# Layer 0 of a two-layer conv-attention kernel: row sums with ones as weights on four column tiles and one transpose, behind the first three steps of the next block; second x loaded later

## The chip, the cores and the metric

The kernel runs on one core of a Trainium2 chip. The metric is the device time of one execution in microseconds (us), the median of three runs. Engines are named as in the profile: PE is TensorE (matmuls), PEld its loading of weights, DVE is VectorE, ACT is ScalarE, POOL is GpSimd, SP is SyncE, which here does nothing but issue transfers. PSUM is the memory that PE writes its products to, one bank a tile.

## What is computed

All data are float32. The input x has 4 images of 128 channels and 64 x 64 = 4096 positions. Layer 0, the one that is changed, is an attention over positions without heads:

```python
def _L0_conv_ref(x, w1, b1, a1, w2, b2, a2, wa, ba, aa):
    e1 = _conv1x1(x, w1, b1, a1).reshape(N, -1, HW)     # 64 x 4096 for each image
    e2 = _conv1x1(x, w2, b2, a2).reshape(N, -1, HW)     # 64 x 4096
    asm = _conv1x1(x, wa, ba, aa).reshape(N, C, HW)     # 128 x 4096
    score = jnp.einsum('nci,ncj->nij', e1, e2)
    score = jax.nn.softmax(score, axis=2)
    out = jnp.einsum('nij,ncj->nci', score, asm)
    return out.reshape(N, C, H, W)
...
x = x + _L0_conv_ref(_gn(x), ...)
t = _to_tokens(x)
t = t + _L1_attn_ref(_ln_t(t), L1_attn_W_kv, L1_attn_q_proj)
t = t + _L1_ffn_ref(_ln_t(t), ...)
```

`_gn` is a group norm, `_ln_t` a layer norm over channels, `_conv1x1` a 1x1 convolution with a leaky ReLU. The softmax's row sums, one for each of the 4096 positions i of an image, are what this change is about. Layer 1 (an attention with cumulative sums, then a mixture of experts) is as before.

## The kernel before

**Blocks and steps.** Layer 0 (`layer0`) walks over 4 images b and, in each, over 8 blocks qb of 512 positions i (`BLK`). A block has 16 steps p (`NPR`), and a step takes 256 positions j. `steps` is the list of all 512 of them and n its index. In a step, `weigh` (L1929) adds to the two accumulators `av` in PSUM: four matmuls of 64 rows, which are 8 matmul instructions, since a float32 matmul is two. Then `probs` (L1909), for the step two ahead, makes the scores `sc` on PE (two matmuls of 64 rows, 4 instructions), their exponentials `pr` on ACT (L1919), and adds them into `acc` on DVE (L1926, a copy at L1923 for a block's first step). `acc` has two halves of 512 columns; the softmax's row sum of a position is the sum of its column over both halves and all 128 partitions. There is no maximum subtracted.

**Block end.** At step 15, `collect` (L1943) moves `av` to `o` (a copy on ACT, L1946, and an addition on DVE, L1947) and adds the halves of `acc` into `sums` (L1950, one buffer). Then `row_sums` runs for the block before, whose name is `done`: four times a 128 x 128 piece of `sums` is loaded as weights and a column of ones is moved through it (L1965), which leaves the sums of 128 positions in one column of `pd`; DVE copies the four columns to `rows` (L1968) and takes `inv`, their reciprocals (L1970). After that comes the block's share of preparing the next image: `project` (L1858: `pe`, `y`, `z`, `e1`, `e2`, with two transfers from SBUF to SBUF on SP) and `value` (L1883: `pa`, `ya`, `za`, `am`), one of each at nearly every block end of images 0 to 2. At the block ends of image 3 there are instead the first keys and tokens of layer 1 (`keys`, L968, matmul `f_pk`, and `tokens`, L961, transposes `f_ltr`). Last comes `finish` (L1973) for `done`: four transposes of `o` into `ptr` (named `otr` in the profile, L1977), and four operations on DVE (L1979) that scale by `inv`, add the input `xr` and write `t`. `fetch` (L1953) then loads `xr` for the block that just ended, and that block becomes `done`.

**Order.** The order on PE is the order of the program text (`manual_schedule` for PE). The orders on DVE, ACT, POOL and SP are chosen by a planner when the program is built, from what it expects to be ready, with the place in the text as the priority; they are then fixed, and each engine runs its own in order.

**Buffers that matter.** PSUM tag `sm` (one bank) holds `pd`, `pa` and, in image 3, the small tiles of layer 1's scan; tag `x` (one bank) holds `pe`, `otr`, `f_ltr` and the scan's rows; tag `kv` (two) holds `sc` and `f_pk`; `av` has one bank for each of its two halves. In SBUF `sums`, `xr` and the input image `x` have one buffer each, `xn` and `o` two, `pr` three. `load_x(b + 1)` writes over the image before, so it waits for the last `normal` (L1850, `xn`) that reads it.

**Scan and close.** In image 3, `point()` runs layer 1's small scan operations at p = 3, 7, 11 and at the block end. `tile_stats` and `close_stats` (L254, L259) take the layer norm's statistics of finished rows of `t`.

**Last block.** Behind the loop, two `later` calls put `row_sums` and `finish` of the very last block behind two `keys`, at the next `point()`.

Of the kernel before, what the change touches and what calls it, by code (L numbers as in the profile page):

```python
# [13 lines left out]
P = 128  # L14
# [3 lines left out]
def conv_attn_hybrid_kernel(  # L18
# [24 lines left out]
    nc = tc.nc  # L43
# [8 lines left out]
    NBLK = N // BLK  # L52
    CPB = BLK // P
# [8 lines left out]
    ident = const.tile([P, P], F32, tag="ident", name="ident")  # L62
# [3 lines left out]
    ones = const.tile([P, 1], F32, tag="ones", name="ones")  # L66
# [179 lines left out]
    rows = resid.tile([P, B * NCH], F32, tag="rows", name="rows")  # L246
# [7 lines left out]
    def tile_stats(pool, b, i):  # L254
        st = pool.tile([P, 6], F32, tag="l1_st", name=f"l1_st_{b}_{i}", bufs=4)
        nc.vector.bn_stats(st, t[:, b * NCH + i, :])
        nc.vector.bn_aggr(ln_mv[:, b, i, :], st)
# [570 lines left out]
    def fast():  # L828
# [18 lines left out]
        def later(delay, fn):  # L847
            env.tasks.append((env.now + delay, fn))

        def point():  # L850
            env.now += 1
            due = [f for at, f in env.tasks if at <= env.now]
            env.tasks = [(at, f) for at, f in env.tasks if at > env.now]
            for f in due:
                f()
# [920 lines left out]
        def layer0(env):  # L1776
            ps, one, big = env.ps, env.one, env.big
            with ExitStack() as l0:
# [5 lines left out]
                def load_x(b):  # L1784
                    xs = one.tile([P, N], F32, tag="x", name=f"x_{b}")
                    parts = 8 if b == 0 else 4
                    for q in range(parts):
                        cols = bass.ts(q, N // parts)
                        eng = nc.scalar if b == 0 and q % 2 else nc.sync
                        eng.dma_start(out=xs[:, cols], in_=x[b, :, cols])  # L1790
                    return xs

                xs_of = {0: load_x(0)}
# [111 lines left out]
                NPR = NCH // 2  # L1905
                steps = [(b, qb, p) for b in range(B) for qb in range(NBLK) for p in range(NPR)]
                acc_of, av_of, o_of, prep = {}, {}, {}, {}

                def probs(b, qb, p):  # L1909
                    e1, e2, _ = made[b]  # L1910
                    cols = bass.ts(qb, BLK)
                    sc = ps.tile([P, 2, BLK], F32, tag="kv", name=f"sc_{b}_{qb}_{p}", bufs=2)
                    for u in range(2):
                        nc.tensor.matmul(  # L1914
                            sc[:, u, :], e2[halves[u], p, :], e1[halves[u], cols],
                            start=True, stop=True,
                        )
                    pr = tmp.tile([P, 2, BLK], F32, tag="pr", name=f"pr_{b}_{qb}_{p}", bufs=3)
                    nc.scalar.activation(pr, sc, AF.Exp)  # L1919
                    if p == 0:  # L1920
                        acc = small.tile([P, 2, BLK], F32, tag="acc", name=f"acc_{b}_{qb}")
                        acc_of[b, qb] = acc
                        nc.vector.tensor_copy(acc, pr)  # L1923
                    else:
                        acc = acc_of[b, qb]
                        nc.vector.tensor_add(acc, acc, pr)  # L1926
                    return pr
# [31 lines left out]

                def row_sums(b, qb):  # L1960
                    o, sums, xr = o_of[b, qb]
                    at = bass.ts(b * NBLK + qb, CPB)
                    pd = ps.tile([P, BLK], F32, tag="sm", name=f"pd_{b}_{qb}")
                    for c in range(CPB):
                        nc.tensor.matmul(  # L1965
                            pd[:, c : c + 1], sums[:, bass.ts(c, P)], ones, start=True, stop=True
                        )
                    nc.vector.tensor_copy(rows[:, at], pd[:, :CPB])  # L1968
                    inv = tmp.tile([P, CPB], F32, tag="inv", name=f"inv_{b}_{qb}")
                    nc.vector.reciprocal(inv, rows[:, at])  # L1970
                    o_of[b, qb] = (o, inv, xr)

                def finish(b, qb):  # L1973
                    o, inv, xr = o_of.pop((b, qb))
                    ptr = ps.tile([P, CPB, C], F32, tag="x", name=f"otr_{b}_{qb}")
                    for c in range(CPB):
                        nc.tensor.transpose(ptr[:, c, :], o[:, bass.ts(c, P)], ident)  # L1977
                    for c in range(CPB):
                        nc.vector.scalar_tensor_tensor(  # L1979
                            out=t[:, b * NCH + qb * CPB + c, :], in0=ptr[:, c, :],  # L1980
                            scalar=inv[:, c : c + 1], in1=xr[:, c, :], op0=ALU.mult, op1=ALU.add,
                        )
# [11 lines left out]
                done, todo = None, []  # L1994
                env.xl_pool = lambda name: tmp.tile([P, CPB, C], F32, tag="xn", name=name)
                for n, (b, qb, p) in enumerate(steps):
                    weigh(b, qb, p, queue.pop(0))
                    if (b, qb) == (0, 0) and p % 2 == 0 and p // 2 + 2 < NBLK:
                        k = p // 2 + 2
                        normal(k)  # L2000
                        project(k)
                        value(k)
                        if k == NBLK - 1:
                            xs_of[1] = load_x(1)
                    if b + 1 < B:
                        first = 1 if b == 0 else 0
                        if qb == first:
                            if p == 0:
                                prep[b + 1] = preparation(b + 1)
                                todo = list(range(NBLK))  # L2010
                            stat, chain, normal, project, value = prep[b + 1]
                            if 1 <= p <= NBLK:
                                stat(p - 1)
                            elif p == NBLK + 1:
                                chain[0]()
                            elif p in (11, 13):
                                chain[(p - 9) // 2]()
                            elif p == 15:
                                normal(0)
                    if b > 0 and 2 <= qb < 6 and p % 2 == 0:  # L2020
                        tile_stats(tmp, b - 1, (qb - 2) * NBLK + p // 2)
                    if b > 0 and (qb, p) == (6, 3):
                        close_stats(b - 1)
                    if b == B - 1 and qb > 0 and p % 4 == 3 and p < NPR - 1:
                        point()
                    if n + 2 < len(steps):
                        queue.append(probs(*steps[n + 2]))
                    if p == NPR - 1:
                        collect(b, qb)
                        if done:  # L2030
                            row_sums(*done)
                        mine = []
                        if todo:
                            left = NBLK - qb
                            mine = [todo.pop(0) for _ in range(-(-len(todo) // left))]
                        for k in mine:
                            _, _, normal, project, value = prep[b + 1]
                            project(k)
                            value(k)
                            if k + 1 < NBLK:  # L2040
                                normal(k + 1)
                            elif b + 2 < B:
                                xs_of[b + 2] = load_x(b + 2)
                            else:
                                env.hold_weights()
                        if b == B - 1:
                            if qb == 0:
                                env.first_rooms()
                                normals(0)
                                tokens(0)  # L2050
                            elif qb <= LAG:
                                for c in range(CPB):
                                    keys(qb - 1, c)
                                tokens(qb)
                            if qb < LAG:
                                normals(qb + 1)
                            point()
                        if done:
                            finish(*done)
                        fetch(b, qb)  # L2060
                        done = (b, qb)
                later(1, lambda: row_sums(*done))
                later(1, lambda: finish(*done))
                keys(LAG, 0)
                keys(LAG, 1)
                point()

        def last_root():
# [257 lines left out]
```

## Time and profile before

| what | value |
|---|---|
| time, median of three runs | 2317.12 us (2316.6 to 2318.71) |
| the profiled execution: its own time | 2323.74 us |
| its span, first to last instruction | 2322.0 us |
| PE busy | 2247.8 us, 97% of the span |
| DVE, ACT, POOL busy | 62%, 47%, 8% |
| mean granted TensorE clock | 0.992 |
| layer 0, up to the last `finish` | about 1533 us of the span |
| `av` matmuls, L1939 | 4096, 978.0 us |
| `sc` matmuls, L1914 | 2048, 534.4 us |
| `pd` matmuls, L1965 | 256, each 167 to 271 ns |
| `otr` transposes, L1977 | 128, each 272 to 329 ns |
| `sums` waits for `pd`, on DVE | 16.3 us in 30 waits |

A PE length in the profile runs from the start of a matmul to its modelled end; matmuls overlap, so a step's cost is read from the distance between starts. In a run of plain steps, the 8 `av` take 1.72 us from first start to the next group's start, and the 4 `sc` take 0.86 us. A form such as 64*128 means weights of 64 rows and 128 columns; PE runs two such side by side, four with 32 columns (128*32), and one at a time with 128*128.

### The profile page before, as it was taken

Reading aid. Unit: us, or ns where it says so; the run is one execution under the profiler, and the core shown is the slowest. Engines: PE = TensorE matmul, PEld = TensorE weight load, DVE = VectorE, ACT = ScalarE, POOL = GpSimd, SP = SyncE. Lnnn points to the kernel's source line nnn. Section 1 sums busy time; section 2 is a strip of 40 time slices with the busy share of each in tenths; the row PEclk is TensorE's granted clock in tenths of the full one; section 3 lists DMA queues with packets and bytes.
Section 4 is the critical chain, followed back from the end, with each engine's and each line's share of the span. In section 5 each row is a group of like instructions: output and inputs, shape, how many; then the busy total and the mean of one; then the engine's idle time right before and its main releaser. Section 6 shows DMA issues by size and latency. Waiting matters only on the chain.

```text
span 2322.0 us, 43150 instructions
## 1 busy us (share of the span) xinstructions
PE 2247.8 (97%) x18352; PEld 1168.5 (50%) x18352; DVE 1444.6 (62%) x2361; ACT 1086.4 (47%) x1324; POOL 175.9 (8%) x364
## 2 busy tenths in 40 slices
PE   7999999999999999999999999999999999999997
PEld 3544444444444444444444444456565556556663
DVE  7666565655665565565556656568777677865623
ACT  2343333433333443334455444455666566566641
POOL 0000000000000000000000000012211222122311
PEclk9999999999999999999999999999999999999989
DMA  2000010000010000000000000011122121114578
GB/s 77 32 12 17 9 45 8 17 8 9 17 45 9 9 17 9 9 25 27 9 5 5 10 5 5 20 44 41 41 58 53 43 59 46 52 47 129 153 279 303
DMA packets 78555, 104.77 MB, mean 45 GB/s; under 512 B 8976, under 2 KB 44816, under 8 KB 78352
## 3 DMA queue, kind: packets, MB, share of 16 engines
q1 hardware_dynamic: 77264, 99.81, 14.0%
q8 instruction: 146, 2.39, 0.4%
q0 software_dynamic: 512, 1.05, 0.2%
q10 hardware_dynamic: 576, 1.05, 0.1%
q14 instruction: 57, 0.47, 0.1%
HBM read 78.55 MB, written 17.04 MB: 41 GB/s over the span
## 4 chain that ended last, share of the span: by engine, by line
PE 86%; DVE 6%; ACT 3%; DMA 3%; issue 1%; SPq 0%; POOL 0%; another core or an unknown queue 0%; ACTq 0%; DVEq 0%; POOLq 0%
PE av L1939 36%; PE sc L1914 18%; PE f_pv L1128 9%; PE f_pk L973 8%; PE f_pt L1151 3%; PE f_po L1174 2%; PE pd L1965 1%; DMA x<-in_x_dram 1%; ACT f_e1a L980 1%; PE pa L1887 1%; PE pe L1861 1%; PE f_po L1186 1%; DVE f_e1a L981 1%; DVE f_e1a L982 1%; PE f_pl L1291 1%
## 5 line engine op out<-in xcount | busy, mean ns | idle before, releaser
L1939 PE MATMUL av<-pr,am 64*128 64x512 f32 x4096 | 978.0, 592 | 2.9 <-ACT pr L1919 2.9
L1919 ACT ACTIVATE pr<-sc 128x1024 f32<-128x1024 f32 x512 | 523.6, 1023 | 782.7 <-PE sc L1914 769.8
L1926 DVE TENSOR_TENSOR acc<-acc,pr 128x1024 f32<-128x1024 f32 x480 | 586.6, 1222 | 485.4 <-ACT pr L1919 481.1
L1939 PEld LDWEIGHTS av<-pr,am 64*128 64x128 f32 x4096 | 401.6, 187 | 472.9 <-issue 457.9
L1914 PE MATMUL sc<-e,e 64*128 64x512 f32 x2048 | 534.4, 591 | 4.7 <-DMA e<-side 4.7
L1914 PEld LDWEIGHTS sc<-e,e 64*128 64x128 f32 x2048 | 201.6, 187 | 236.6 <-issue 229.0
L1128 PE MATMUL f_pv<-f_held,f_ama 128*32 128x256 f32 x4096 | 242.7, 387 | 5.5 <-ACT f_e1a L980 4.5
L973 PE MATMUL f_pk<-f_held,f_ama 128*128 128x512 f32 x512 | 234.9, 603 | 0.0
L1133 ACT ACTIVATE f_amb<-f_pv 128x1024 f32<-128x1024 f32 x128 | 130.8, 1023 | 141.7 <-PE f_pv L1128 140.9
L981 DVE TENSOR_TENSOR f_e1a<-f_e1a,f_held 128x1024 f32<-128x1024 f32 x128 | 157.5, 1231 | 46.6 <-ACT f_e1a L980 46.2
L980 ACT ACTIVATE f_e1a<-f_pk 128x1024 f32<-128x1024 f32 x128 | 129.9, 1025 | 117.8 <-PE f_pk L973 57.8
L1128 PEld LDWEIGHTS f_pv<-f_held,f_ama 128*32 128x32 f32 x4096 | 131.3, 111 | 102.2 <-issue 15.1
L982 DVE TENSOR_REDUCE f_e1a<-f_e1a 128x8 f32<-128x1024 f32 x128 | 155.3, 1218 | 3.5
L973 PEld LDWEIGHTS f_pk<-f_held,f_ama 128*128 128x128 f32 x512 | 92.5, 190 | 109.1 <-issue 101.4
L1092 POOL COPY f_held<-f_e1a 32x32 f32<-32x32 f32 x128 | 30.5, 238 | 924.1 <-DVE f_e1a L1074 563.3
L1151 PE MATMUL f_pt<-f_amb,f_held 128*32 128x128 f32 x1920 | 83.0, 276 | 0.8 <-ACT f_amb L1133 0.8
L918 POOL MEMSET f_held<- 128x1024 f32 x1 | 1.0, 956 | 1036.3 <-DVE xn L1852 1036.3
L1151 PEld LDWEIGHTS f_pt<-f_amb,f_held 128*32 128x32 f32 x1920 | 59.9, 109 | 10.3 <-issue 5.2
L1192 DVE TENSOR_TENSOR t<-t,f_po 128x512 f32<-128x512 f32 (+1 forms) x33 | 22.1, 671 | 55.6 <-PE f_po L1186 55.6
L956 ACT ACTIVATE f_xl<-t,ln_nb,ln_rs 128x128 f32<-128x128 f32 x128 | 52.8, 490 | 0.8 <-PE pa L1887 0.8
L1272 ACT ACTIVATE f_x<-t,f_gnb,f_grs 128x128 f32<-128x128 f32 x126 | 51.3, 482 | 0.4 <-DVE f_gnb L1253 0.4
L1923 DVE COPY acc<-pr 128x1024 f32<-128x1024 f32 x32 | 22.2, 694 | 39.3 <-ACT pr L1919 39.3
(287 smaller groups left out, 1776.6 us busy)
## 6 DMA issues: line engine op xcount, KB each, us to landing
f_e2a<-f_rd SPq DMA_DIRECT2D x128, 128.0 KB, 2.9
xr<-in_xtok_dram SPq DMA_DIRECT2D x32, 256.0 KB, 3.0
f_table<-f_x SPq DMA_DIRECT2D x62, 128.0 KB, 1.8
out_dram<-t SPq DMA_DIRECT2D x14, 512.0 KB, 3.8
x<-in_x_dram SPq DMA_DIRECT2D x12, 512.0 KB, 7.0
e<-e SPq DMA_DIRECT2D x32, 128.0 KB, 2.2
f_ama<-f_rd SPq DMA_DIRECT2D x16, 256.0 KB, 3.8
f_e1b<-f_rd SPq DMA_DIRECT2D x16, 256.0 KB, 6.0
```

Source lines behind the costliest of these rows:

```text
L956: nc.scalar.activation(xl[:, c, :], t[:, b * NCH + i, :], AF.Identity, bias=ln_nb[:, b, i : i + 1], scale=ln_rs[:, b, i : i + 1],)
L973: nc.tensor.matmul(pk[:, i, :], xt_at(n)[:, bass.ts(c, P)], env.wks[:, bass.ts(i, BLK)], start=True, stop=True,)
L980: nc.scalar.activation(flat, pk.rearrange("p i x -> p (i x)"), AF.Silu)
L981: nc.vector.tensor_mul(ks, ks, env.qb)
L982: nc.vector.tensor_reduce(s[:, (n % GB) * CPB + c, :], ks, AX.X, ALU.add)
L1128: nc.tensor.matmul(pv[a * CH : (a + 1) * CH, i, :], xt_at(m)[:, bass.ts(c * NA + i, CH)], env.wvs[:, bass.ts(a, HH * C)], start=True, stop ...
L1133: nc.scalar.activation(env.amb[:, bass.ts(c, HD)], pv.rearrange("p i x -> p (i x)"), AF.Silu)
L1151: nc.tensor.matmul(env.pt[i * CH : (i + 1) * CH, :], lhs, rhs, start=i not in env.begun, stop=False, skip_group_check=True,)
L1914: nc.tensor.matmul(sc[:, u, :], e2[halves[u], p, :], e1[halves[u], cols], start=True, stop=True,)
L1919: nc.scalar.activation(pr, sc, AF.Exp)
L1926: nc.vector.tensor_add(acc, acc, pr)
L1939: nc.tensor.matmul(av, am[h, j, :], pr[h, u, :], start=(j == 0), stop=(j == NCH - 1))
```

## The change

`row_sums` is split in two. The first part loads a 128 x 32 array of ones as weights (a broadcast of the column `ones`) and moves the four 128-column pieces of `sums` through it. Each piece's result goes to another 32 partitions of `pd`, so the four matmuls use four column tiles of PE. DVE then copies the 128 x 128 result back into `sums`. The second part, `row_turn`, transposes that once on PE and copies every 32nd column to `rows`, then takes the reciprocals. The two parts and `finish` leave the block end: they run behind `weigh` of steps 1, 2 and 3 of the next block, one in each, for the block that has just ended. For the last block they lie around the two `keys`. The load of the second image moves in the text from step 10 of the first block to step 13.

```diff
                 def row_sums(b, qb):
                     o, sums, xr = o_of[b, qb]
-                    at = bass.ts(b * NBLK + qb, CPB)
                     pd = ps.tile([P, BLK], F32, tag="sm", name=f"pd_{b}_{qb}")
                     for c in range(CPB):
+                        rows_ = slice(c * (P // CPB), (c + 1) * (P // CPB))
                         nc.tensor.matmul(
-                            pd[:, c : c + 1], sums[:, bass.ts(c, P)], ones, start=True, stop=True
-                        )
-                    nc.vector.tensor_copy(rows[:, at], pd[:, :CPB])
+                            pd[rows_, :P], ones.to_broadcast([P, P // CPB]), sums[:, bass.ts(c, P)],
+                            start=True, stop=True,
+                        )
+                    nc.vector.tensor_copy(sums[:, :P], pd[:, :P])
+                    o_of[b, qb] = (o, sums, xr, pd)
+
+                def row_turn(b, qb):
+                    o, sums, xr, pd = o_of[b, qb]
+                    at = bass.ts(b * NBLK + qb, CPB)
+                    nc.tensor.transpose(pd[:, P : 2 * P], sums[:, :P], ident)
+                    nc.vector.tensor_copy(rows[:, at], pd[:, P : 2 * P : P // CPB])
                     inv = tmp.tile([P, CPB], F32, tag="inv", name=f"inv_{b}_{qb}")
                     nc.vector.reciprocal(inv, rows[:, at])
                     o_of[b, qb] = (o, inv, xr)
...
                         value(k)
-                        if k == NBLK - 1:
-                            xs_of[1] = load_x(1)
...
+                    if done and 1 <= p <= 3:
+                        (row_sums, row_turn, finish)[p - 1](*done)
                     if n + 2 < len(steps):
                         queue.append(probs(*steps[n + 2]))
+                    if n == NPR - 3:
+                        xs_of[1] = load_x(1)
                     if p == NPR - 1:
                         collect(b, qb)
-                        if done:
-                            row_sums(*done)
...
-                        if done:
-                            finish(*done)
                         fetch(b, qb)
                         done = (b, qb)
-                later(1, lambda: row_sums(*done))
                 later(1, lambda: finish(*done))
                 keys(LAG, 0)
+                row_sums(*done)
                 keys(LAG, 1)
+                row_turn(*done)
                 point()
```

## The prediction

> **What bounds the kernel.** I read the chain of waits first.
>
> ```profile
> PE 86%; DVE 6%; ACT 3%; DMA 3%; issue 1%; SPq 0%; POOL 0%; another core or an unknown queue 0%; ACTq 0%; DVEq 0%; POOLq 0%
> ```
>
> PE ends nearly everything, so the change is worth what it does to the order of starts on PE. Next come PE's starts around one block end of image 0 (columns: start, length, engine, line, operation, count; distances between starts are what counts).
>
> ```profile
> 263.83 1.02 PE L1914 MATMUL sc<-e,e 64*128 64x512 f32 x4
> 264.78 1.05 PE L1965 MATMUL pd<-ones,sums 128*128 128x1 f32 x8
> 265.69 1.10 PE L1861 MATMUL pe<-xn,w 128*128 128x512 f32 x2
> 266.78 1.13 PE L1887 MATMUL pa<-was,xn 128*128 128x128 f32 x8
> 267.75 0.60 PE L1977 MATMUL otr<-ident,o 128*128 128x128 f32 x4
> 268.28 1.99 PE L1939 MATMUL av<-pr,am 64*128 64x512 f32 x8
> 270.10 1.02 PE L1914 MATMUL sc<-e,e 64*128 64x512 f32 x4
> ```
>
> PE has no gap. Against the plain pace (sc 0.86, av 1.72) the block end costs 0.09 on the way out of the 64-row form (0.95 - 0.86), pd 0.91, pe 1.09, pa 0.97, otr 0.53, and 0.10 on the way back (av 1.82 instead of 1.72): 3.69 us. pd is eight weight loads at 0.11 each.
>
> **What is left of a block end.** In the first block pe and pa stand alone between steps:
>
> ```profile
> 27.61 1.12 PE L1861 MATMUL pe<-xn,w 128*128 128x512 f32 x2
> 28.57 1.05 PE L1887 MATMUL pa<-was,xn 128*128 128x128 f32 x8
> 29.55 1.13 PE L1914 MATMUL sc<-e,e 64*128 64x512 f32 x4
> ```
>
> So 0.09 + 0.96 + 0.98 + 0.10 = 2.13, and the removal is worth 3.69 - 2.13 = 1.56 us. The next av needs the old accumulators copied out: ACT ends its copy at 264.61 and DVE its addition at 265.33, while PE would come to av at 264.78 + 1.94 = 266.72. That stays hidden; without pe and pa it would cost some 0.6.
>
> **What three visits cost.** Nothing is hidden here: each visit stands in PE's order between av and sc, and pays the way out and back. The trace has a lone transpose in just that place:
>
> ```profile
> 1386.07 1.88 PE L1939 MATMUL av<-pr,am 64*128 64x512 f32 x8
> 1387.88 0.33 PE L1026 MATMUL f_str<-ident,f_e1a 128*128 128x128 f32 x1
> 1388.14 1.13 PE L1914 MATMUL sc<-e,e 64*128 64x512 f32 x4
> 1389.11 1.45 PE L1939 MATMUL av<-pr,am 64*128 64x512 f32 x6
> ```
>
> av takes 1.81, the transpose 0.26, sc 0.97: 0.09 + 0.26 + 0.11 = 0.46. That is row_turn. finish alone is otr where nothing precedes it, 0.59 (1222.56 to 1223.15 below), with 0.20 around it: 0.78. The new row_sums has no row of its own; the nearest has the same form, weights of 32 columns and 128 moved:
>
> ```profile
> 1539.78 1.08 PE L1151 MATMUL f_pt<-f_amb,f_held 128*32 128x128 f32 x32
> 1540.68 0.51 PE L1174 MATMUL f_po<-f_amb,f_e2a 128*32 128x128 f32 x12
> ```
>
> 32 instructions in 0.90. Their single starts lie in fours, 7 ns apart, the second four 0.135 behind the first and the others 0.109 apart. pd's eight are two fours: 0.135 + 0.02 + 0.20 from the last start to the next form's (as from f_eo's last, 2230.33, to f_htr, 2230.53) = 0.355, with 0.20 around it 0.55. Bounds: if pairs on one column tile follow each other, 8 x 0.107 = 0.86, 0.5 more; below 0.3 it can't go, since two fours of 128 columns and a drain remain. I take 0.355, the same form. Sum of visits: 0.55 + 0.46 + 0.78 = 1.79.
>
> The Trainium skill's "TensorEngine Tiling (Array Packing)", Key Properties, says that changing the tiling mode drains the engine; that speaks against this change, which makes three such pairs of changes out of one, and the rows price it at 0.20 a pair. The skill's "TensorE: Matmul & The Clock Gate", Part 3, gives a packed set as one matmul's duration plus some 4 ns a tile; two sets one after the other, at 0.273 each, would be an estimated 0.57 instead of 0.355, or 31 x 0.21 = 6.7 us more in all.
>
> **Sum by kinds of block.** Images 0 to 2 have 22 block ends with one pe and pa: 22 x (1.79 - 1.56) = **+5.1**. The end of the second block has two of each; there otr waits for pe's bank (1.1) behind ACT, and pd to the last otr take 7.04 (126.54 to 133.58). Without pd and otr 4.2 remain (0.96, 0.98, 1.27, 1.0): -2.83 + 1.79 = **-1.0**. Image 3 looks like this:
>
> ```profile
> 1212.85 1.05 PE L1965 MATMUL pd<-ones,sums 128*128 128x1 f32 x8
> 1213.77 7.11 PE L973 MATMUL f_pk<-f_held,f_ama 128*128 128x512 f32 x16
> 1220.72 0.60 PE L965 MATMUL f_ltr<-ident,f_xl 128*128 128x128 f32 x4
> 1222.56 0.66 PE L1977 MATMUL otr<-ident,o 128*128 128x128 f32 x4 [1.25 <-ACT f_ama L966]
> 1223.15 1.99 PE L1939 MATMUL av<-pr,am 64*128 64x512 f32 x8
> ```
>
> Here otr needs the bank that f_ltr holds until ACT has copied it. That wait goes: 0.91 + 1.85 + 0.59 less 0.55 for f_ltr and 0.05 for a cold f_pk is 2.75, against 1.79: -0.95. What is late next is ACT: behind the keys it has four normals (1.64) and a table load (1.28) and starts the next pr at 1226.27. Its keys can start only 0.5 earlier (it waited 0.47 for f_pk), so pr ends at 1226.7 while av of step 2 wants it at 1226.3: a new wait of 0.5 (0 to 0.5). Five blocks at -0.45: **-2.3**. Image 3's first end has f_ltr alone (1.31): -2.22 + 1.79 = **-0.4**. In the seventh, f_ur keeps the wait for the bank: **-0.3**. In three blocks the scan has an operation at step 3, and finish shares its way out and back: **-0.6**. At the very end pd, otr, keys, pd, otr take 6.19 (1526.37 to 1532.56); keys 1.8, pd 0.5, keys 1.8, turn 0.13, otr 0.7 make 4.9, and I keep **-1.2**, since sums is free on DVE right behind the last acc (1525.3).
>
> That is +5.1 - 1.0 - 2.3 - 0.4 - 0.3 - 0.6 - 1.2 = -0.7. Layer 0 also has four PE waits of its own: 1.2 at 331 and 0.7 at 693 (DVE stands in stats for an image's transfer, and acc and pr come late), and 0.7 each at 458 and 819 (two table loads of close_stats). Four t operations (1.4 us of DVE) leave the queue ahead of them; close_stats moves with finish into the image's first block, where DVE is emptier. They may go, or grow by as much: -3.3 to +3. I take **-0.9**.
>
> **DVE, ACT, queues.** DVE gets one copy of 128x128 a block (0.29 by f_e1b at L1168), and loses its 0.54 wait of sums for pd; it idles 1.35 us of each 2.58 us step, so this costs nothing. The one new wait on PE is row_turn's for that copy. PE is 0.96 + 1.72 + 0.09 = 2.8 us from the sc behind pd to the transpose; the copy needs 0.29 and at most the 1.22 of an acc in progress. ACT gets nothing. On SP, fetch's transfer only becomes free earlier, and finish passes no queue. The **second x** goes at zero: its transfers were issued at 54.51, right behind the xn that frees the buffer (53.93), although their place in the text is behind av of 62.28, and the first xr went at 10.71 with a place behind 83. The place in the text does not hold SP; the buffer does. If it did hold, the PE wait between 64 and 75 (0.48 + 2.28 + 0.75, DVE in stats while z, ya and e are due) would go: -3.5.
>
> All in all -0.7 - 0.9 = -1.6 us on the profiled 2323.74 (span 2322.0); on the median of 2317.12 that is **2315.5**. Own range 2310.5 to 2321: the ACT wait and all four stalls gone (-2.5, -2.4), or the stalls doubled (+3.9) and a tenth of the visits at the upper price.
>
> **Rivals.** (1) *The x load really comes later*, -3.5 more: 2312. For it: the text moved; against: 10.71 and 54.51. Chance 0.18. (2) *row_turn waits on DVE.* If the planner's order puts the copy behind acc of step 3, it ends 2.15 + 1.22 + 0.29 = 3.7 behind sc's start (sc to acc by 261.25, 262.35, 263.40), 0.9 after PE comes to the transpose, with av and sc queued behind it. In all 31 blocks +28, 2343; it makes the kernel slower by more than 0.2% from seven blocks on, and in ten gives 2323. For it: the order is fixed beforehand and DVE is behind in the blocks where an image lands; against: pd is done 2 us before that pr. Chance 0.17. (3) *The four column tiles do not run together*: 0.86 instead of 0.355, 31 x 0.5 = +15.6, 2331; f_pt and f_eo speak against. Chance 0.08. The forecast has 0.52; 0.05 is for none of these.
>
> **How the numbers follow.** About 0.2% (4.6 us) is what a measurement of this kernel tells from no change: 2312.5 to 2321.7. The forecast spreads 0.13 faster, 0.33 same, 0.06 slower; rival 1 gives 0.13 faster and 0.05 same; rival 2 0.13 slower and 0.04 same; rival 3 0.08 slower; the rest 0.03 faster, 0.02 slower. Together 0.29, 0.42, 0.29. The range 2309.5 to 2323 leaves out rival 3, most of rival 2 and little below.
>
> **What would show it.** Starts on PE: pe right behind sc at block ends, 2.13 there; visits of 0.55, 0.46 and 0.78; pd's eight starts in two fours; no idle time before row_turn; otr's waits for f_ama gone and up to 0.5 on pr in image 3; x's second transfer still at 54.5. A visit over 0.7 for pd, waits before row_turn, or an unmoved block end would make this wrong.

## The result, and the profile after

| | before | after |
|---|---|---|
| time, median of 22 runs each on one chip | 2320.03 us (2313.64 to 2325.55) | 2321.34 us (2317.01 to 2326.75) |
| after / before | | 1.0005, 95% interval 0.9997 to 1.0013 |
| profiled execution: own time, span | 2323.74, 2322.0 | 2318.04, 2316.3 |
| layer 0, up to the start of the first `f_pv` (L1128) | 1532.56 | 1533.28 |

The change makes no difference that can be measured. The forecast was that, at 2315.5 against the 2317.12 shown, -1.6; measured is +1.3 between the medians.

The profiled execution after is 5.7 us shorter, but not in layer 0. From the first `f_pv` to the end, where both programs have the same work, the two profiles need 789.45 and 783.03, and the seven other profiles below spread over 783.0 to 790.5. So layer 0 is compared by its own end, which is a far finer ruler: a regular block repeats to 0.01 us from block to block and from profile to profile. From here on a block is the distance from its first `av` to the first `av` of the next, and blocks are numbered 0 to 31 through the four images.

PE's waits between 20 and 1535 us add up to 18.0 before and 10.6 after, while layer 0 got no shorter: what was saved in waits was spent on PE. The next view is PE's timeline at the same block end of image 0 that the prediction showed, and the three visits behind it (start, length, engine, line, operation, count):

```profile
266.55 1.02 PE L1914 MATMUL sc<-e,e 64*128 64x512 f32 x4
267.50 1.12 PE L1861 MATMUL pe<-xn,w 128*128 128x512 f32 x2
268.46 1.05 PE L1887 MATMUL pa<-was,xn 128*128 128x128 f32 x8
269.45 1.99 PE L1939 MATMUL av<-pr,am 64*128 64x512 f32 x8
...
272.13 1.88 PE L1939 MATMUL av<-pr,am 64*128 64x512 f32 x8
273.94 0.42 PE L1965 MATMUL pd<-sums,ones 128*32 128x128 f32 x8
274.30 1.13 PE L1914 MATMUL sc<-e,e 64*128 64x512 f32 x4
275.26 1.88 PE L1939 MATMUL av<-pr,am 64*128 64x512 f32 x8
277.07 0.33 PE L1975 MATMUL pd<-ident,sums 128*128 128x128 f32 x1
277.33 1.13 PE L1914 MATMUL sc<-e,e 64*128 64x512 f32 x4
278.29 1.88 PE L1939 MATMUL av<-pr,am 64*128 64x512 f32 x8
280.11 0.66 PE L1985 MATMUL otr<-ident,o 128*128 128x128 f32 x4
280.69 1.13 PE L1914 MATMUL sc<-e,e 64*128 64x512 f32 x4
```

At the block end `pe` now follows `sc` directly: 0.09 + 0.96 + 0.99 + 0.10 = 2.14. Each visit shows the same two surcharges: the `av` ahead of it takes 1.81 or 1.82 instead of 1.72, the `sc` behind it 0.96 instead of 0.86. Between them `pd` takes 0.36, the transpose 0.26, `otr` 0.59 (0.589 by its single starts). A regular block went from 44.90 to 45.15.

Block 6 is one of the two in which the input of a later image arrives. PE's timeline there (in brackets idle time and what ended it):

```profile
320.41 1.88 PE L1939 MATMUL av<-pr,am 64*128 64x512 f32 x8
324.16 0.33 PE L1975 MATMUL pd<-ident,sums 128*128 128x128 f32 x1 [1.87 <-DVE sums L1969]
```

and DVE's at the same place:

```profile
319.05 1.22 DVE L1926 TENSOR_TENSOR acc<-acc,pr 128x1024 f32<-128x1024 f32 x1
321.95 1.96 DVE L1829 BATCH_NORM_STATS2 stats<-x 128x6 f32<-128x512 f32 x3 [1.68 <-DMA x<-in_x_dram]
323.83 0.27 DVE L1969 COPY sums<-pd 128x128 f32<-128x128 f32 x1
```

`pd` is ready at 319.5, but in DVE's fixed order its copy stands behind three `stats`, and these wait for the image's transfer. PE comes to the transpose at 322.2 and stands until the copy is done.

Image 3, the same place as in the prediction:

```profile
1228.17 0.60 PE L965 MATMUL f_ltr<-ident,f_xl 128*128 128x128 f32 x4
1228.70 1.99 PE L1939 MATMUL av<-pr,am 64*128 64x512 f32 x8
...
1233.20 0.42 PE L1965 MATMUL pd<-sums,ones 128*32 128x128 f32 x8
1233.55 1.13 PE L1914 MATMUL sc<-e,e 64*128 64x512 f32 x4
1234.71 1.99 PE L1939 MATMUL av<-pr,am 64*128 64x512 f32 x8
1236.63 0.33 PE L1975 MATMUL pd<-ident,sums 128*128 128x128 f32 x1
```

with ACT's `pr` at the same place:

```profile
1233.63 2.12 ACT L1919 ACTIVATE pr<-sc 128x1024 f32<-128x1024 f32 x2
```

`otr`'s wait of 1.25 for `f_ama` is gone from the block end. In its place `sc` at 1233.55 takes 1.16 to the next start and `av` 1.92, which is 0.2 and 0.1 more than in image 0 above: PE waits a little for `pr`, the first of which ACT starts only at 1233.63, behind the keys, and ends at about 1234.65.

### The profile page after: what moved, and what is told of

It reads as the page before. It is cut to its first block, busy times and chain, and to the rows that moved or that the text cites. A ratio compares the mean times of both kernels' runs of the same rounds, so it can differ in the third digit from the quotient of the medians.

```text
span 2316.3 us, 43180 instructions
## 1 busy us (share of the span) xinstructions
PE 2249.5 (97%) x18384; PEld 1132.1 (49%) x18384; DVE 1455.5 (63%) x2393; ACT 1086.5 (47%) x1324; POOL 177.1 (8%) x364
## 4 chain that ended last, share of the span: by engine, by line
PE 89%; DVE 4%; ACT 3%; DMA 2%; issue 1%; SPq 0%; ACTq 0%; DVEq 0%
PE av L1939 38%; PE sc L1914 20%; PE f_pv L1128 9%; PE f_pk L973 8%; PE f_pt L1151 3%; PE f_po L1174 2%; PE pe L1861 1%; PE pa L1887 1%; PE f_po L1186 1%; DMA x<-in_x_dram 1%; PE otr L1985 1%; PE f_pl L1291 1%; PE f_ltr L965 1%; ACT f_e1a L980 1%; PE f_ph L1665 1%
## 5 line engine op out<-in xcount | busy, mean ns | idle before, releaser
L1939 PEld LDWEIGHTS av<-pr,am 64*128 64x128 f32 x4096 | 395.3, 187 | 475.0 <-issue 462.9
L1914 PEld LDWEIGHTS sc<-e,e 64*128 64x128 f32 x2048 | 190.5, 187 | 211.0 <-issue 202.4
L1128 PE MATMUL f_pv<-f_held,f_ama 128*32 128x256 f32 x4096 | 241.3, 385 | 5.5 <-ACT f_e1a L980 4.5
L1128 PEld LDWEIGHTS f_pv<-f_held,f_ama 128*32 128x32 f32 x4096 | 130.7, 111 | 101.2 <-issue 13.4
L1887 PEld LDWEIGHTS pa<-was,xn 128*128 128x128 f32 x256 | 34.3, 196 | 17.8 <-issue 14.4
```

What stands on the lines that cost most here:

```text
L1128: nc.tensor.matmul(pv[a * CH : (a + 1) * CH, i, :], xt_at(m)[:, bass.ts(c * NA + i, CH)], env.wvs[:, bass.ts(a, HH * C)], start=True, stop ...
L1887: nc.tensor.matmul(pa[:, c, :], xn[:, bass.ts(c, P)], was, start=True, stop=True)
L1914: nc.tensor.matmul(sc[:, u, :], e2[halves[u], p, :], e1[halves[u], cols], start=True, stop=True,)
L1939: nc.tensor.matmul(av, am[h, j, :], pr[h, u, :], start=(j == 0), stop=(j == NCH - 1))
```

## The experiments

One theory stood at the start. **Theory V**: each visit costs 0.2 us for leaving the 64-row form and coming back, so what the cheaper arithmetic gains, the three visits spend. Its rivals put the cost into the new arithmetic itself, or into waits on DVE. Each experiment's layer 0 is read at the start of its first `f_pv`; the ratio is to the kernel before, in runs on the same chip. The edits are shown against the changed kernel, with less important parts left out.

| kernel | layer 0, us | against before | ratio of times, 95% interval |
|---|---|---|---|
| before | 1532.56 | | |
| after | 1533.28 | +0.72 | 1.0005, 0.9997 to 1.0013 |
| 1: two visits | 1522.23 | -10.33 | 0.9944, 0.9930 to 0.9957 |
| 2: at the block's end | 1514.74 | -17.82 | 0.9929, 0.9916 to 0.9943 |
| 3: move only | 1533.03 | +0.47 | 1.0006, 0.9997 to 1.0015 |
| 4: x really held | 1535.81 | +3.25 | 1.0012, 1.0003 to 1.0021 |
| 5: copy on ACT | 1528.67 | -3.89 | 0.9987, 0.9978 to 0.9996 |
| 6: mixed | 1508.54 | -24.02 | 0.9904, 0.9888 to 0.9919 |
| 7: all at the end | 1507.78 | -24.78 | 0.9894, 0.9879 to 0.9909 |

Each row is one profile, and not all of a difference is the edit's. In eight of the nine profiles the granted TensorE clock, the share of full speed that PE is allowed, is 0.5 for a stretch of 3.4 us in layer 0 (experiment 1 has none, experiment 4 two), which costs up to 1.7. These are the kernel before, in two windows, and the changed one (window, length, PE busy and matmuls, granted clock, DMA share, GB/s):

```profile
70.26:73.67 3.41, 3.41 (x20) 1.00 0.13 29
1484.13:1487.55 3.42, 3.42 (x9) 0.50 0.00 0
```

```profile
70.26:73.67 3.41, 3.41 (x10) 0.50 0.07 16
```

The stretch lies in block 31 before, in block 0 with the change and in experiments 3, 5, 6 and 7, in block 17 in experiment 2, and in blocks 1 and 14 in experiment 4. Each begins during PE waits that add up to 1.8 to 3.8 us, or at most 1.3 behind them. But waits of 1.8 to 2.6 occur without such a stretch too, so what brings it about is open.

**Experiment 1: two visits instead of three.**

```diff
-                    if done and 1 <= p <= 3:
-                        (row_sums, row_turn, finish)[p - 1](*done)
+                    if done and p == 1:
+                        row_sums(*done)
+                    if done and p == 2:
+                        row_turn(*done)
+                        finish(*done)
```

> The changed kernel, with finish in the same visit as row_turn (behind step 2) instead of one of its own behind step 3. Theory V (a visit costs 0.09 on the way out, 0.10 on the way back, and an own start of some 0.1 behind the transpose): turn and otr together take 0.16 + 0.53 + 0.20 = 0.89 instead of 0.46 + 0.78 = 1.24, -0.35 in 28 blocks and -0.15 in the three where finish shared the scan's step: layer 0 10 us shorter, time 2311 against 2321 for the changed kernel on the same chip. Rival (the price lies in the instructions, the switches are hidden by the weight loads): 0 to -2. Rival (DVE): four t operations one step earlier make acc late, a new PE wait of up to 1 in each block: +10 or more.

PE's timeline, the joint visit:

```profile
272.55 1.88 PE L1939 MATMUL av<-pr,am 64*128 64x512 f32 x8
274.36 0.33 PE L1975 MATMUL pd<-ident,sums 128*128 128x128 f32 x1
274.53 0.60 PE L1985 MATMUL otr<-ident,o 128*128 128x128 f32 x4
275.06 1.13 PE L1914 MATMUL sc<-e,e 64*128 64x512 f32 x4
```

The transpose is followed after 0.17 and not 0.26, `otr` after 0.53, and only one pair of surcharges is paid. Every regular block is 44.80 instead of 45.15, -0.35 as worked out, with the same instructions on PE. Layer 0 is 11.05 shorter than with the change, of which 0.99 arose in block 0, where this profile has no stretch at half clock, and 0.30 ahead of it; blocks 1 to 31 give 9.8 against the expected 10. Theory V holds. No wait on DVE came with it in the regular blocks, so that rival is out.

**Experiment 2: the new arithmetic, not moved.** Images 0 to 2 have all three parts at the block's end; `pd` takes a bank of tag `kv` there, because `pa` has the one of `sm`.

```diff
-                    if done and 1 <= p <= 3:
+                    if done and b == B - 1 and 1 <= p <= 3:
                         (row_sums, row_turn, finish)[p - 1](*done)
...
                         collect(b, qb)
+                        if done and b < B - 1:
+                            row_sums(*done, at_end=True)
...
+                        if done and b < B - 1:
+                            row_turn(*done)
+                            finish(*done)
                         fetch(b, qb)
```

> The new arithmetic without the move in images 0 to 2: row_sums, row_turn and finish are at the block's end again (pd in a bank of sc's pair, so that it does not collide with pa); image 3 as in the changed kernel. Theory V: the end of a regular block is 0.09 + 0.36 + 0.96 + 0.98 + 0.16 + 0.53 + 0.10 = 3.18 against 3.69 before and 2.13 + 1.79 = 3.92 in the changed kernel: block 44.4 against 44.90 and 45.15, layer 0 about 16 us shorter than with the change (22 x -0.74, the waits of row_turn where an image lands, 4 us, gone, old waits of 2 and the bank wait of the second block, 1.1, back). Rival (the arithmetic is what costs and the move is neutral): block at 45.0 or more. Rival (row_turn waits for DVE, which stands in the addition of the accumulators and in acc): 0.3 to 1.2 a block lost again, block 44.7 to 45.6.

PE's timeline at a block end:

```profile
262.06 1.02 PE L1914 MATMUL sc<-e,e 64*128 64x512 f32 x4
263.01 0.42 PE L1968 MATMUL pd<-sums,ones 128*32 128x128 f32 x8
263.37 1.13 PE L1861 MATMUL pe<-xn,w 128*128 128x512 f32 x2
264.33 1.05 PE L1887 MATMUL pa<-was,xn 128*128 128x128 f32 x8
265.22 0.27 PE L1978 MATMUL pd<-ident,sums 128*128 128x128 f32 x1
265.33 0.60 PE L1988 MATMUL otr<-ident,o 128*128 128x128 f32 x4
265.86 1.99 PE L1939 MATMUL av<-pr,am 64*128 64x512 f32 x8
```

The block end costs 0.09 + 0.36 + 0.96 + 0.89 + 0.11 + 0.53 + 0.10 = 3.04, even less than the 3.18 expected, since instructions of the 128-column form follow each other without a gap. A regular block is 44.25. Both rivals are out: the arithmetic saves 0.65 a block where it stands among its like, and `row_turn` never waits for its copy, which DVE has made while PE is in `pe` and `pa`.

Against the change layer 0 gained 18.5, and would have gained more but for blocks 9 and 17 (46.78 and 48.39). ACT's timeline in block 9 shows why:

```profile
446.78 1.02 ACT L1919 ACTIVATE pr<-sc 128x1024 f32<-128x1024 f32 x1 [3.53 <-PE sc L1914]
447.82 1.28 ACT L260 ACT_TABLE_LOAD   x1
451.43 0.32 ACT L260 ACTIVATE ln_rs<-ln_mv,eps 128x32 f32<-128x32 f32 x1 [2.32 <-DVE ln_mv L257]
451.77 1.28 ACT L1919 ACT_TABLE_LOAD   x1
```

`close_stats` (L259) takes its root when an image's last rows are finished, and with `finish` at the block's end that is one block later. In ACT's fixed order the root stands ahead of the next `pr` and waits 2.32 for the last `ln_mv`. PE waits 2.26 for that `pr` in both blocks; the 1.61 that block 17 is longer is the stretch at half clock, from 811.58.

**Experiment 3: the old arithmetic, moved.**

```diff
-                            pd[rows_, :P], ones.to_broadcast([P, P // CPB]), sums[:, bass.ts(c, P)],
-                            start=True, stop=True,
+                            pd[:, c : c + 1], sums[:, bass.ts(c, P)], ones, start=True, stop=True
...
-                    if done and 1 <= p <= 3:
-                        (row_sums, row_turn, finish)[p - 1](*done)
+                    if done and p == 1:
+                        row_sums(*done)
+                    if done and p == 3:
+                        finish(*done)
```

> The move without the new arithmetic: sums as weights on the vector of ones, eight weight loads, behind step 1 of the next block; no row_turn; finish behind step 3. Theory V: the pd visit takes 0.91 + 0.20 = 1.11 against 0.55 + 0.46 = 1.01, so a regular block is 44.90 - 1.56 + 1.11 + 0.78 = 45.23 (45.15 with the change), and the two blocks where an image lands lose row_turn's wait of 2 each: layer 0 within +-2 of the changed kernel. Rival (the arithmetic is what slows the changed kernel): a regular block at 44.8 or less, layer 0 8 us or more shorter than with the change.

PE's timeline:

```profile
274.23 1.05 PE L1965 MATMUL pd<-ones,sums 128*128 128x1 f32 x8
275.21 1.13 PE L1914 MATMUL sc<-e,e 64*128 64x512 f32 x4
```

`pd` takes 0.98 here and 0.91 at the old block end, where the weights of `pe` follow it. A regular block is 45.32 (45.23 expected). Blocks 6 and 14 are 45.32 too, so without `row_turn` nothing on PE waits for DVE there. Layer 0 is 0.25 shorter than with the change, inside the +-2 of theory V; the rival's -8 is out. Experiments 2 and 3, the changed kernel and the one before make a square, a regular block in each:

| | at the block's end | behind the steps |
|---|---|---|
| sums as weights | 44.90 | 45.32 |
| ones as weights, one transpose | 44.25 | 45.15 |

Read along the rows: the move costs 0.42 with the old arithmetic and 0.90 with the new, which needs one visit more. Read down: the arithmetic is worth 0.65 in place and 0.17 moved. The change takes the square's diagonal.

**Experiment 4: the second x really held back.** The kernel before has `load_x(1)` at step 10 of the text and the changed one at step 13, but every engine has the same order of instructions up to the end of block 0 in both profiles, and the four transfers are issued at 54.51 in both. Here is SP with the change:

```profile
54.51 1.81 SPq L1790 DMA_DIRECT2D x<-in_x_dram  x4
```

In this experiment a dependency holds them until the `acc` that the text writes at step 13 is done. Since `probs` runs two steps ahead, that is the `acc` of step 15, the block's last, and the transfers are issued at 77.06.

```diff
-                        eng.dma_start(out=xs[:, cols], in_=x[b, :, cols])
+                        d = eng.dma_start(out=xs[:, cols], in_=x[b, :, cols])
+                        if b == 1:
+                            tc.add_manual_dep(d.ins, held[0].ins.name, ...)
...
-                        nc.vector.tensor_add(acc, acc, pr)
+                        held[:] = [nc.vector.tensor_add(acc, acc, pr)]
```

> The changed kernel, with the second image's load really held until the acc of step 13 is done (a dependency added to its four transfers). Theory H (the first block's PE waits of 3.5 to 4.6 come from DVE standing in stats while the first image's z, ya and e are due): the first block goes from 58.8 to 54.5 to 55.3; eight stats stand in the second block then, where row_turn may wait up to 2 for its copy: layer 0 1.5 to 4.5 us shorter. Rival (the waits of the first block come from its own preparation, not from stats): first block unchanged within 1 us, second block longer, layer 0 the same or longer.

Block 0 fell from 58.83 to 54.19, block 1 rose from 49.46 to 55.36. PE's timeline at the start of block 1:

```profile
84.59 1.97 PE L1949 MATMUL av<-pr,am 64*128 64x512 f32 x5 [3.80 <-DVE o L1957]
```

and DVE's ahead of it:

```profile
80.87 1.29 DVE L1837 BATCH_NORM_STATS2 stats<-x 128x6 f32<-128x512 f32 x2 [3.11 <-DMA x<-in_x_dram]
82.08 0.68 DVE L1933 COPY acc<-pr 128x1024 f32<-128x1024 f32 x1
82.67 1.28 DVE L1837 BATCH_NORM_STATS2 stats<-x 128x6 f32<-128x512 f32 x2
83.86 0.67 DVE L1957 TENSOR_TENSOR o<-o,av 128x512 f32<-128x512 f32 x1
```

Theory H is right about block 0: its waits come from DVE standing in `stats`. It is wrong about what follows. The stall did not go to `row_turn`; it moved to the addition that frees the accumulators, where PE waits 3.80. Layer 0 came out 2.5 longer than with the change: 1.3 longer in blocks 0 and 1 together, 1.5 in block 14, and 0.3 shorter elsewhere. The clock has a share in that: the stretch at half clock in block 0 is gone, and there are two others, from 85.59 in block 1, behind the wait of 3.80, and from 689.75 in block 14, where `row_turn`'s own wait (1.95) is not longer than with the change (2.05).

**Experiment 5: the copy of `pd` on ACT.**

```diff
-                    nc.vector.tensor_copy(sums[:, :P], pd[:, :P])
+                    nc.scalar.copy(sums[:, :P], pd[:, :P])
```

> The changed kernel, with the copy of pd to sums on ACT instead of DVE. Theory W (row_turn's waits of about 2 in the two blocks where an image lands, 47.09 and 47.27 long, are DVE's: the copy stands behind three stats that wait for a transfer): both blocks 45.15, layer 0 4.1 shorter, and up to 1.5 of it lost in image 3, where ACT is late behind the keys. Rival (acc and pr come late there anyway, as in the kernel before with its waits of 1.2 and 0.7): both blocks 45.8 to 46.3, layer 0 2.2 shorter. Rival (the waits are not the copy's): both blocks unchanged.

PE's timeline in block 6:

```profile
319.85 1.88 PE L1939 MATMUL av<-pr,am 64*128 64x512 f32 x8
321.66 0.33 PE L1975 MATMUL pd<-ident,sums 128*128 128x128 f32 x1
```

Both blocks are 45.15: theory W holds to the hundredth, and the old waits did not come back. Layer 0 is 4.61 shorter than with the change, 4.06 of it in these two blocks, the rest in block 0 and ahead of it. Image 3 is unchanged, so ACT's copy cost nothing there either.

**Experiment 6: all three at the block's end in images 0 to 2, two visits elsewhere.** Behind an image's last block the parts are visits, which puts `close_stats` back into the image's first block; image 3 has two visits as in experiment 1. `row_sums` takes its bank as an argument, else it is as in experiment 2.

```diff
+                    visits = b == B - 1 or qb == 0
+                    if done and visits and p == 1:
+                        row_sums(*done)
+                    if done and visits and p == 2:
+                        row_turn(*done)
+                        finish(*done)
...
                         collect(b, qb)
+                        if done and not visits:
+                            row_sums(*done, "kv")
...
+                        if done and not visits:
+                            row_turn(*done)
+                            finish(*done)
```

> All three at the block's end in images 0 to 2 as in the second experiment, except behind the last block of an image, where they are two visits (behind steps 1 and 2 of the next block); two visits in image 3 too. Theory T (the waits of 2.5 and 4.1 in blocks 9 and 17 of the second experiment are close_stats: its root comes one block later there and stands in ACT's queue, waiting for the last ln_mv): blocks 9 and 17 go from 46.78 and 48.39 to 44.25, blocks 8 and 16 lose 0.4 to 0.8 each, image 3 gains 2.1 as in the first experiment: layer 0 7.5 shorter than in the second experiment, f_pv at 1507, time 0.989 of before. Rival (the waits come from DVE's longer queue at block ends): blocks 9 and 17 stay above 46, layer 0 1.5 to 3 shorter.

Blocks 9 and 17 are 44.25, blocks 8 and 16 rose by 0.78 and 0.76, image 3 gained 2.1: theory T holds. Layer 0 is 6.2 shorter than in experiment 2 and not 7.5; 0.7 of the difference is block 14 (45.00 instead of 44.26), another 0.3 the time ahead of block 0. Of the 4.1 that block 17 lost in experiment 2, 1.6 was the clock's.

**Experiment 7: at the block's end in image 3 too.** The rest is as in experiment 6.

```diff
+                    visits = qb == 0 or (b, qb) == (B - 1, NBLK - 1)
...
                                     keys(qb - 1, c)
+                                    if c == 0:
+                                        row_turn(*done)
+                                        finish(*done)
```

> As the sixth experiment, and in blocks 1 to 6 of image 3 all three at the block's end too, row_turn and finish behind the first of the four keys. Theory V: 0.36 + 0.13 + 0.53 = 1.02 instead of 0.55 + 0.89 = 1.44 for two visits, -0.4 in the four blocks without a shared visit and -0.2 in two: layer 0 2 shorter than in the sixth, time 0.988 of before. Rival (DVE has the keys' products and sums in its queue there, the t operations come late and f_ltr waits for the bank): 0.5 to 1.5 a block more, layer 0 3 to 9 longer than in the sixth.

PE's timeline at a block end of image 3 and in the steps behind it:

```profile
1247.35 0.43 PE L1968 MATMUL pd<-sums,ones 128*32 128x128 f32 x8
1247.70 1.98 PE L973 MATMUL f_pk<-f_held,f_ama 128*128 128x512 f32 x4
1249.53 0.27 PE L1978 MATMUL pd<-ident,sums 128*128 128x128 f32 x1
1249.63 0.60 PE L1988 MATMUL otr<-ident,o 128*128 128x128 f32 x4
...
1261.88 1.99 PE L1939 MATMUL av<-pr,am 64*128 64x512 f32 x8 [0.70 <-ACT pr L1919]
```

The visits are gone from the steps, but behind a block end with keys PE now reaches `av` of step 2 earlier and waits 0.70 for `pr`. Blocks 26 to 29 are 50.77, 50.78, 50.77 and 51.75 against 50.75, 50.75, 50.74 and 51.72 in experiment 6: the gain is eaten whole. Blocks 25 and 30 keep 0.64 and 0.53. Layer 0 is 0.8 shorter, where 2 were expected; the rival's wait for the bank did not appear. This version and the sixth are about 1% faster than the kernel before, which the change had left level; their intervals overlap, so which is the better one is not shown.

## Why the prediction was right

The forecast of no measurable change held, and so did the shape of the reasoning: a small price in many blocks against gains in image 3. That the sum came so close is partly luck, as the last three paragraphs of this section show. The sum against what layer 0 did, block by block:

| term | predicted | measured |
|---|---|---|
| 22 blocks with one `pe` and `pa` | +5.1 (0.23 each) | +5.6 (0.254 each) |
| four PE waits of layer 0 | -0.9 | +0.8 |
| second block | -1.0 | -0.7 |
| image 3, first block | -0.4 | -0.2 |
| image 3, the rest and the tail | -4.4 | -5.9 |
| second x, block 0 | 0 | +1.1 |
| sum | -1.6 | +0.7 |

**Removal at the block end**, 1.56: measured 3.69 - 2.14 = 1.55. **The three visits**, 0.55 + 0.46 + 0.78 = 1.79: measured 0.36, 0.26 and 0.59 with 0.20 around each, 1.80. Experiment 1 changes nothing but the number of visits and shows the price again, 0.35 for one: 0.20 of surcharges, 0.09 of the transpose and 0.06 of `otr`, which are followed sooner.

**The form of `pd`.** The first four of its eight instructions start at 273.940, 273.946, 273.953 and 273.960, the next four at 274.072 to 274.092, and the next form at 274.295: two fours, as in `f_pt`, and 0.355 in all. Rival 3, column tiles one behind the other, is out, and so is the estimate of 0.57 from the Trainium skill's "TensorE: Matmul & The Clock Gate", Part 3: the second set does not wait for the end of the first, which the profile models at 274.236, but starts 0.13 behind it. The rule of "TensorEngine Tiling (Array Packing)", Key Properties, that a change of tiling mode drains the engine, fits the runs, which show a surcharge of 0.09 to 0.10 at each change of form out of the 64-row form and back, though not what it consists of.

**The four PE waits** are the step that failed, in sign. The waits of 1.2 and 0.7 at 331 and 693 are gone, as hoped, but `row_turn`'s own wait took their place: blocks 6 and 14 are 1.94 and 2.12 longer than their neighbours, where they had been 1.28 and 0.77 longer. That is the wait that rival 2 named, for the copy in DVE's fixed order, in two of 31 blocks, though behind `stats` and not behind an `acc`, and at about 2.0 a block instead of its 0.9. (By that 0.9, ten blocks would give 2324.5, not the 2323 that the prediction has.) The prediction said that the copy needs 0.29 "and at most the 1.22 of an acc in progress"; what stood ahead of it was three `stats` with 1.96 of work, which had begun 1.68 late for want of their data. Experiment 5 moves the copy off DVE and both waits vanish. The other two waits, at `close_stats`, changed by -1.2 together with its move into the image's first block.

**Image 3** gained 1.5 more than predicted, and here two things that the prediction did not have cancel. Its sum prices the tail by its length alone and leaves out that the visits for block 30 stand in block 31: steps 1 to 3 there take 0.55, 0.45 and 0.60 more, +1.60. Against that, the first step of block 31 takes 4.38 before and 2.68 with the change, -1.70, since the kernel before spends it at half clock. With the tail itself, -1.46 for the predicted -1.2, block 31 comes to -1.55. The gain over the forecast is elsewhere: a new wait on ACT was set at 0.5 in each of five blocks; it is 0.3, and the first of them has none, since no keys ended the block before it (block 25: -1.04; 26 to 28: -0.60).

**Second x.** The text's place holds nothing, as argued: order and time of issue are the same before and after. The +1.1 of block 0 is not the edit's doing: the instructions of this block and their order are the same in all profiles but experiment 4's, and they need 57.74 to 58.83. PE is 0.35 behind the kernel before at 70.15, where the stretch at half clock begins, 1.93 at its end, and 1.10 once the kernel before has had its own wait of 0.56 for `e` at 74.77. The waits differ a little too (58.30 in experiment 2, without such a stretch in block 0); why was not tried. Rival 1's price of 3.5 comes out against the kernel before, 57.74 - 54.19 = 3.55, but experiment 4 shows that a real hold, as late as it has it, does not keep the gain.

**The clock.** So the two profiles hold one stretch at half clock each, in different places, and +0.7 contains both. Without them the change would be an estimated 0.72 - 1.1 + 1.7 = +1.3 in layer 0, which is as little to be told from nothing in the medians.

## What to carry to other kernels

Count the visits, not only the instructions: work of another matmul form that is spread over single steps pays the way out and back each time, here 0.2 us of PE against 0.36, 0.26 and 0.59 of work, while the same work at the block's end, beside other instructions off the 64-row form, paid no surcharge of its own (experiment 2). When a change does two things, cost them apart: here a good edit (-0.65 a block) and a bad one (+0.90) cancelled, and the total alone would have condemned both. Before a new PE instruction is made to wait for a vector copy, look at what the fixed order puts ahead of that copy, and above all whether that in turn waits for a transfer.

## What the runs showed of the hardware that was not expected

- Two sets of four 32-column matmuls overlap: 0.36 from the first start to the next form's, where the eight instructions have modelled lengths of 0.27 to 0.30 each.
- A lone 128 x 128 transpose costs 0.26 to the next form's start ahead of `sc`, 0.16 to 0.17 ahead of `otr` in a visit of its own (experiment 1), and 0.11 in the middle of other 128-column work (experiment 2).
- ACT copied `pd` (128 x 128) to SBUF in 0.27, the same as DVE's 0.27 in the same place.
- In layer 0 the granted clock was 0.5 for 3.4 us nine times in nine profiles, always within or close behind PE waits that add up to 1.8 to 3.8 us; other waits of 1.8 to 2.6 passed without it.
